# Input loads as steps of the planned order in the last stage of a graph network kernel

## The chip, the cores and the metric

The kernel runs on one core of a Trainium2 chip. The metric is the device time of one launch in microseconds; the figure to compare is the median of several runs. The engines are PE (matrix multiply), ACT (activations), DVE (vector operations), POOL (GpSimd) and SP (which only issues transfers here).

## The reference

x is 128 graphs of 128 nodes with 128 channels (float32); adj is a 0/1 adjacency matrix for each graph. Four layers follow one another, each of the form x = x + layer(relu(layernorm(x)), adj), and in each a softmax over a node's neighbours is taken.

```python
# --- layer 0: pairwise |xi - xj| scores, BatchNorm over all graphs, softmax, and then
y = (y - mg) / jnp.sqrt(vg + EPS) * gg + beg      # mg, vg over all graphs and nodes
y = _leaky(y)
out = jnp.concatenate([x, y], axis=2) @ Wt.T + bt
# --- layer 1: 8 heads of 32, then one head of 128 (masked softmax, ELU)
# --- layer 2: one head of 128 (masked softmax, ELU)
# --- layer 3: a bilinear score for each edge type, chosen by adj; softmax; two projections
```

Layer 0 needs means over all graphs, so everything up to y is done for all graphs first. What comes after y is separate for each graph: the rest of layer 0 and layers 1 to 3.

## The kernel before

The work falls into stages. First come the statistics of the pairs of nodes and the scores of layer 0; they leave in DRAM, for each group of 4 graphs (GC), four inputs of the last stage: xb (x with a bias, 256 KB), m (the mask, 128 KB), y (256 KB) and h (the normalised x, transposed, 256 KB). There are 32 groups. The last stage, `layers_01`, begins at about 1737 us. It takes a group from these four inputs to its output, through the rest of layer 0 and through layers 1, 2 and 3.

**A group's steps at the start**, with the lines of the profile: ACT makes yl from yt, scaled and shifted (L1866); DVE does the leaky step (L551); PE adds two products for each graph in po, ht times the first half of Wt and yl times the second (L1872, L1875); DVE adds xg and makes x1 (L1881); DVE takes mean and variance into mv (L1669, L1671); ACT makes the reciprocal root rs from them (L1674, L1675); POOL makes xn in two steps (L1678, L1679); PE transposes it (L1686) and ACT copies it out as hTc (L1689); PE projects it to pf (L1896); DVE splits pf in four instructions (L1905 to L1908) and ACT spreads the parts over heads as f1d and fl (L1917). On the side, DVE makes x1h (L1840). Then for each graph there are a product z (L1770), exponentials (L1776, L1779), the mask step p on DVE (L1781) and the sums (L1810). The output is written from SP at L2027.

**The order of the work.** Each group is a Python generator. Before a step it yields the engine, a cost in us, the buffers that the step takes and those that it frees. A list scheduler, `in_order` (L64), holds up to 8 groups under way (Z_UNDER_WAY), always picks the step that can begin first by these costs, and lets that generator emit its instructions. The order of emission is the order in which PE, ACT, DVE and POOL execute: each of these engines runs its instructions strictly in that order, and an instruction whose input has not come holds up those behind it. SP is not in that list (ORDERED): its requests are ordered by the framework. A step ends for its follower after a gap for its engine:

```python
AFTER = dict.fromkeys((PE, ACT, DVE, POOL), 0.2) | {DMA: 2.2}
...
begin = max([free_at[engine], c["ready"], *(events[e] for e in c["after"])])
```

Besides steps a generator can yield "fork" (start a side chain), "join" (go on when its side chains are done), "done" (set an event) and "after" (the next step waits for that event). Buffers are named: "ps" and "pz" are PSUM, "t", "w", "v" and others are SBUF tiles.

**The inputs.** `load` allocates xg, mask, yt and ht (3, 10, 3 and 3 buffers) and asks for them on SP in this order. It is a plain function: `group(g)` calls it for g + 1 when it starts, and neither the transfer nor its buffers appear in the plan. As eight groups start at plan time 0, the loads of groups 1 to 8 are written at the front. The inputs of group 0 lie in buffers of their own, filled before the stage (`first_in`).

Of the kernel before, what the change touches and what calls it, by code (L numbers as in the profile page):

```python
# [27 lines left out]
GC = 4  # L28
# [6 lines left out]
Z_T, Z_W, Z_P, Z_F, Z_O, Z_M = 30, 13, 4, 4, 6, 10  # L35
Z_KEPT = {"ps": 1, "t": 4, "w": 2, "v": 1, "vals": 1}
# [20 lines left out]
PE, ACT, DVE, POOL, DMA = "PE", "ACT", "DVE", "POOL", "DMA"  # L57
# [3 lines left out]
AFTER = dict.fromkeys((PE, ACT, DVE, POOL), 0.2) | {DMA: 2.2}  # L61
# [112 lines left out]
def kernel(ctx: ExitStack, tc: tile.TileContext, x, adj, w, out):  # L174
    nc = tc.nc
    NB = x.shape[0]
# [370 lines left out]
    def inputs_01(g):  # L547
        return xb_d[g], mask_d[g], y_d[g], h_d[g]
# [1080 lines left out]
    def layers_01(first_in):  # L1629

        with tc.tile_pool(name="c_in", bufs=3) as c_in, tc.tile_pool(
# [19 lines left out]
            def tile_t(name):  # L1651
                return c_t.tile([P, GC, P], F32, tag="t", name=name)
# [97 lines left out]
            loaded = dict(first_in)  # L1750

            def load(g):
                tiles = [
                    c_in.tile([P, GC, P], dtype, tag=name, name=name, bufs=n)
                    for name, dtype, n in (("xg", F32, 3), ("mask", BF16, Z_M), ("yt", F32, 3), ("ht", F32, 3))
                ]
                for dst, src in zip(tiles, inputs_01(g)):
                    nc.sync.dma_start(dst, src)
                loaded[g] = tiles

            def with_bias3(x3):
                yield POOL, 1.3, "", ""
                nc.gpsimd.tensor_tensor(x3, x3, bcast(pb_bc, 1, GC), ALU.add)
# [93 lines left out]

            def group(g):
                b0 = g * GC
                xg, mask, yt, ht = loaded.pop(g)  # L1860
                if g + 1 < NB // GC and g + 1 not in loaded:
                    load(g + 1)
                res = {}
                yield ACT, 0.72, "t", ""
                yl = tile_t("yl")
                nc.scalar.activation(yl, yt, AF.Identity, bias=y_bi, scale=y_sc)  # L1866
                yield DVE, 0.82, "", ""
# [3 lines left out]
                for i in range(GC):  # L1871
# [3 lines left out]
                    nc.tensor.matmul(  # L1875
                        po[:, i, :], yl[:, i, :], wtT[:, 1, :], start=False, stop=i == GC - 1
                    )
                yield "join",
                yield DVE, 0.66, "t", "ps"
                x1 = tile_t("x1")  # L1880
                nc.vector.tensor_tensor(x1, po, xg, ALU.add)  # L1881

# [20 lines left out]
                f = c_v.tile([P, 2 * P], BF16, tag="f", name="f")  # L1903
# [122 lines left out]
                nc.gpsimd.tensor_tensor(xh, xh, x3, ALU.add)  # L2026
                nc.sync.dma_start(out_t[:, b0 : b0 + GC, :], xh)  # L2027

            for g in range(2):
                if g not in loaded:  # L2030
                    load(g)
            in_order(
                [partial(group, g) for g in range(NB // GC)], Z_UNDER_WAY,
                {"ps": 4, "pz": 2, "t": Z_T, "w": Z_W, "vals": Z_P, "f": Z_F, "v": Z_O},
                Z_KEPT,
            )

    def layers(simple, first_in):
# [457 lines left out]
    with tc.If(nc.values_load(types[0:1, 0:1]) < 1) as only_01:  # L2496
        layers_01({0: early})
# [42 lines left out]
```

## Time and profile before

| | |
|---|---|
| median of 3 runs | 2680.19 us (2677.42 to 2680.2) |
| the profiled execution's own time | 2677.98 us |
| its span, with 51543 instructions | 2676.1 us |
| busy over the span: PE, DVE, ACT, POOL | 93%, 91%, 81%, 61% |
| DMA, mean over the span | 122.62 MB, 46 GB/s |
| last stage: first request of an input | 1736.98 us |
| last stage: first and last output request | 1868.64 and 2670.8 us |
| mean granted clock of PE | 0.972 |

The span is the time from the first to the last instruction of one profiled execution; its own time is 1.9 us longer. In rows of the trace a name such as "yl<-yt" says which tile is written from which. "Idle before, releaser" says how long the engine had done nothing before an instruction and which engine's result, or which transfer, ended that. In the views by stage, each engine has its busy time and its number of instructions, followed by the clock granted to PE (1 is full), the share of time in which the 16 DMA engines were busy, and GB/s.

### The profile page before, as it was taken

The numbers are of one execution on the slowest core, as the hardware profiler recorded it, in microseconds if no ns is written. First come the engines' busy times: TensorE is split into PE (matmuls) and PEld (weight loads), VectorE is DVE, ScalarE is ACT, GpSimd is POOL, SyncE is SP. The second block draws the span as 40 slices with busy tenths as digits, with TensorE's granted clock in tenths as the row PEclk, the third lists the DMA queues.
The fourth block names the chain that finished last, engine by engine and source line by source line (L and its number), as shares of the span: only waits on it lengthen the run. The fifth ranks groups of instructions, "written<-read, shape, count | busy, mean of one in ns | idle before, by whom it ended". The sixth has DMA issues, their size and how long they took to land. (4 is left out here: it accounts for less than half of the span.)

```text
span 2676.1 us, 51543 instructions
## 1 busy us (share of the span) xinstructions
PE 2489.0 (93%) x19585; PEld 1559.4 (58%) x19595; DVE 2423.4 (91%) x4638; ACT 2160.1 (81%) x3537; POOL 1632.1 (61%) x922
## 2 busy tenths in 40 slices
PE   8999999999999999799999999778998989898888
PEld 3433444444333333577777777566776767676766
DVE  9999999999999998889998998678988898889886
ACT  8999999999999998466665666468777777787885
POOL 8999999999999999544444443022333333333234
PEclk9999999999999999899999999979998999999999
DMA  3000000000000000322322221040211111110001
GB/s 103 24 24 24 24 24 24 24 24 24 24 24 24 24 23 21 113 86 83 100 92 88 88 84 44 22 133 10 62 35 48 37 37 45 46 45 25 10 2 34
DMA packets 135731, 122.62 MB, mean 46 GB/s; under 512 B 10865, under 2 KB 102450, under 8 KB 135474
## 3 DMA queue, kind: packets, MB, share of 16 engines
q1 hardware_dynamic: 134754, 118.89, 14.6%
q8 instruction: 158, 2.59, 0.4%
q14 instruction: 99, 0.81, 0.1%
q10 hardware_dynamic: 720, 0.33, 0.0%
HBM read 73.05 MB, written 46.14 MB: 45 GB/s over the span
## 5 line engine op out<-in xcount | busy, mean ns | idle before, releaser
L727 POOL TENSOR_TENSOR d<-he 128x2016 f32<-128x2016 f32 (+1 forms) x272 | 961.0, 3560 | 17.7 <-PE ph L752 14.2
L752 PE MATMUL ph<-d,w1T 128*64 128x512 f32 (+1 forms) x4096 | 912.7, 596 | 16.3 <-DVE six L764 9.8
L731 ACT ACTIVATE d<-d 128x2048 f32<-128x2048 f32 (+1 forms) x448 | 833.1, 1888 | 18.0 <-POOL d L727 17.0
L752 PEld LDWEIGHTS ph<-d,w1T 128*64 128x64 f32 x4096 | 322.8, 136 | 545.8 <-issue 471.1
L722 DVE SCALAR_TENSOR_TENSOR d<-pt,he 128x2048 f32<-128x2048 f32 x240 | 543.2, 2271 | 4.6 <-PE ph L752 4.4
L764 DVE BATCH_NORM_STATS2 six<-ph 128x6 f32<-128x512 f32 (+1 forms) x704 | 438.0, 677 | 11.7 <-PE ph L752 11.4
L1678 POOL TENSOR_TENSOR xn<-xo,mv 128x512 f32<-128x512 f32 x64 | 74.0, 1156 | 324.0 <-DVE mv L1671 257.1
L1083 PE MATMUL pl<-its,it 128*128 128x128 f32 x1280 | 171.4, 282 | 2.8 <-DVE its L1076 2.7
L758 ACT ACTIVATE ph<-ph 128x1008 f32<-128x1008 f32 x160 | 159.7, 998 | 11.9 <-PE ph L752 11.6
L1083 PEld LDWEIGHTS pl<-its,it 128*128 128x128 f32 x1280 | 155.5, 194 | 20.7 <-DVE its L1076 7.9
L1781 DVE SCALAR_TENSOR_TENSOR p<-z,mask 128x1024 f32<-128x1024 f32 x124 | 147.7, 1210 | 8.0 <-ACT z L1779 7.7
L1037 ACT ACTIVATE d<-diff 128x640 f32<-128x640 f32 x128 | 89.7, 701 | 79.4 <-PE diff L1028 79.4
L1679 POOL TENSOR_TENSOR xn<-xn,rs 128x512 f32<-128x512 f32 x96 | 110.9, 1155 | 51.3 <-ACT rs L1675 39.5
L1015 POOL TENSOR_TENSOR base<-base,own_d 128x512 f32<-128x512 f32 x32 | 43.4, 1357 | 158.3 <-PE ph L1041 77.4
L1073 ACT CAST it<-pi 128x640 f32<-128x640 bf16 x128 | 86.6, 691 | 64.7 <-PE pi L1070 64.7
L1028 PE MATMUL diff<-inc,h 128*128 128x320 bf16 x768 | 128.6, 304 | 5.8 <-DVE inc L944 3.9
L1779 ACT ACTIVATE z<-z 128x1024 f32<-128x1024 f32 x128 | 129.0, 1008 | 4.1
L944 DVE SCALAR_TENSOR_TENSOR inc<-in_row,row 128x8 bf16<-128x8 f32 (+12 forms) x512 | 126.0, 315 | 1.9 <-PE in_row L935 1.8
L1045 ACT ACTIVATE z<-ph,h_bi,h_sc 128x320 f32<-128x320 f32 x128 | 77.9, 618 | 54.4 <-PE ph L1041 52.5
L1678 POOL TENSOR_TENSOR xn<-x,mv 128x512 f32<-128x512 f32 x32 | 37.0, 1157 | 136.9 <-DVE mv L1671 72.6
L1810 PE MATMUL va<-p,vals 128*32 128x128 f32 x2048 | 107.6, 283 | 8.3 <-DVE vals L1795 4.9
L1076 DVE TENSOR_TENSOR its<-pi,s 128x640 f32<-128x640 bf16 x128 | 102.2, 809 | 13.1 <-ACT it L1073 12.7
(326 smaller groups left out, 5309.3 us busy)
## 6 DMA issues: line engine op xcount, KB each, us to landing
ht<-h SPq DMA_DIRECT2D x64, 256.0 KB, 2.7
n<-ln_xn SPq DMA_DIRECT2D x32, 256.0 KB, 2.4
h<-he SPq DMA_DIRECT2D x32, 256.0 KB, 2.6
adj<-in_adj SPq DMA_DIRECT2D x32, 256.0 KB, 3.0
xn<-n SPq DMA_DIRECT2D x32, 256.0 KB, 2.6
xb<-in_x SPq DMA_DIRECT2D x32, 256.0 KB, 3.0
xb<-xb SPq DMA_DIRECT2D x32, 256.0 KB, 2.0
xg<-xb SPq DMA_DIRECT2D x32, 256.0 KB, 2.7
```

What stands on the lines that cost most here:

```text
L722: nc.vector.scalar_tensor_tensor(dv, own, 0.0, later, ALU.max, ALU.max if is_larger else ALU.subtract)
L727: nc.gpsimd.tensor_tensor(dv, later, own, ALU.subtract)
L731: nc.scalar.activation(d[:, 0 : 4 * n], d[:, 0 : 4 * n], AF.Abs, accum_out=sums[:, g, k : k + 1] if on_act else None,)
L752: nc.tensor.matmul(ph[64 * a : 64 * a + 64, t, 0:n], wt, x_, start=part == 0, stop=not is_larger or part == 3,)
L758: nc.scalar.activation(ph[:, :, 0:n], ph[:, :, 0:n], AF.Square, accum_out=squares[:, g, k : k + 1])
L764: nc.vector.bn_stats(six[g][:, 2 * by_bn.index((i, q)) + t, :], ph[:, t, 0:n])
L944: nc.vector.scalar_tensor_tensor(inc[:, :, e : e + n], in_row[:, :, 0:n], float(k + 1), row[:, :, 0:n], ALU.is_equal, ALU.subtract,)
L1028: nc.tensor.matmul(diff[:, a, 0 : SLOT_N // 2], h[:, i, :], inc[:, a * SLOT_N // 2 : (a + 1) * SLOT_N // 2], start=m == 0, stop=m == 2,)
L1083: nc.tensor.matmul(made["pl"][:, i, :], it[:, k, :], its[:, k, :], start=k == 0, stop=k == 4)
L1678: nc.gpsimd.tensor_tensor(xn, x, bcast(mv[:, :, 0], 2, P), ALU.subtract)
L1779: nc.scalar.activation(z, z, AF.Exp, scale=1.0 - SLOPE)
L1781: nc.vector.scalar_tensor_tensor(p, z, 1.0, bcast(mask[:, i, :], 1, NH), ALU.max, ALU.mult)
```

## The change

All of it lies in `layers_01`. `load` becomes a side chain with a step of its own on an engine "DMA" of the plan: it costs 2.9, takes a buffer "in", of which there are three, and sets the event ("loaded", g) at its end. `group(g)` forks the load of g + 1; groups other than 0 wait in the plan for their own event before their first step, and give "in" back with x1. The order of the four requests becomes yt, ht, xg, mask. The "join" ahead of x1 is dropped. The loop that called `load(1)` before planning goes, and the plan takes ACT as free only from 1.5.

```diff
             def load(g):
+                yield DMA, 2.9, "in", ""
                 tiles = [
                     c_in.tile([P, GC, P], dtype, tag=name, name=name, bufs=n)
                     for name, dtype, n in (("xg", F32, 3), ("mask", BF16, Z_M), ("yt", F32, 3), ("ht", F32, 3))
                 ]
-                for dst, src in zip(tiles, inputs_01(g)):
-                    nc.sync.dma_start(dst, src)
+                parts = list(zip(tiles, inputs_01(g)))
+                for k in (2, 3, 0, 1):
+                    nc.sync.dma_start(*parts[k])
                 loaded[g] = tiles
+                yield "done", ("loaded", g)
...
             def group(g):
                 b0 = g * GC
-                xg, mask, yt, ht = loaded.pop(g)
-                if g + 1 < NB // GC and g + 1 not in loaded:
-                    load(g + 1)
+                in_slot = "" if g in first_in else "in"
+                if in_slot:
+                    yield "after", ("loaded", g)
+                if g + 1 < NB // GC:
+                    yield "fork", load(g + 1)
                 res = {}
                 yield ACT, 0.72, "t", ""
+                xg, mask, yt, ht = loaded.pop(g)
                 yl = tile_t("yl")
...
-                yield "join",
-                yield DVE, 0.66, "t", "ps"
+                yield DVE, 0.66, "t", "ps " + in_slot
                 x1 = tile_t("x1")
                 nc.vector.tensor_tensor(x1, po, xg, ALU.add)
...
-            for g in range(2):
-                if g not in loaded:
-                    load(g)
             in_order(
                 [partial(group, g) for g in range(NB // GC)], Z_UNDER_WAY,
-                {"ps": 4, "pz": 2, "t": Z_T, "w": Z_W, "vals": Z_P, "f": Z_F, "v": Z_O},
-                Z_KEPT,
+                {"ps": 4, "pz": 2, "t": Z_T, "w": Z_W, "vals": Z_P, "f": Z_F, "v": Z_O, "in": 3},
+                Z_KEPT, dict.fromkeys(AFTER, 0.0) | {ACT: 1.5},
             )
```

## The prediction, made before the changed kernel was run

> **What bounds the kernel now.** I read the page for the shares, then busy time by stage, then the waits of the last stage's first 25 us, then ACT and DVE there in order of time. Busy time by stage (each engine: us, instructions):
>
> ```profile
> core 0: us, PE busy (x) PEld busy (x) DVE busy (x) ACT busy (x) POOL busy (x), PEclk, DMA share, GB/s
> 1736.50:1749.00 12.50, 9.38 (x41) 8.82 (x42) 2.39 (x4) 4.53 (x5) 0.00 (x0) 0.51 0.77 261
> 1749.00:1761.00 12.00, 5.95 (x48) 5.76 (x48) 9.34 (x40) 4.68 (x11) 3.45 (x4) 0.78 0.95 294
> 1761.00:1773.00 12.00, 8.30 (x99) 6.06 (x99) 10.73 (x29) 9.25 (x22) 7.68 (x7) 0.78 0.28 92
> 1773.00:1783.00 10.00, 8.50 (x87) 5.56 (x87) 9.41 (x20) 9.74 (x19) 1.04 (x1) 0.67 0.09 26
> 1783.00:2640.00 857.00, 757.00 (x8387) 598.11 (x8386) 750.53 (x1670) 676.16 (x1488) 288.23 (x264) 0.95 0.12 33
> 2640.00:2676.10 36.10, 26.45 (x178) 21.31 (x176) 15.98 (x35) 14.84 (x28) 14.44 (x14) 0.92 0.17 47
> ```
>
> From 1783 to 2640 the stage runs on compute: PE 88%, DVE 88%, DMA 12%. The first 25 us are the reverse: DMA 77 to 95%, DVE 2.39 us of 12.5. Waits from 1736.5 to 1761 (total, times, longest):
>
> ```profile
> POOL xn L1678 <- DMA ht<-h: 17.3, 1, 17.3
> ACT yl L1866 <- DMA yt<-y: 13.4, 7, 3.3
> DVE yl L551 <- ACT yl L1866: 10.9, 5, 3.5
> DVE x L1881 <- DMA xg<-xb: 2.3, 1, 2.3
> ```
>
> By the tile views these are nearly all the waits for inputs in the stage: yt has only those seven. The mechanism is in the order of time (start, duration; ACT, then DVE):
>
> ```profile
> 1738.03 0.81 ACT L1866 ACTIVATE yl<-yt,y_bi,y_sc 128x512 f32<-128x512 f32 x1
> ...
> 1754.95 0.81 ACT L1866 ACTIVATE yl<-yt,y_bi,y_sc 128x512 f32<-128x512 f32 x1 [2.71 <-DMA yt<-y]
> 1757.13 0.81 ACT L1866 ACTIVATE yl<-yt,y_bi,y_sc 128x512 f32<-128x512 f32 x1 [1.37 <-DMA yt<-y]
> 1757.85 0.28 ACT L1674 ACTIVATE rs<-mv,eps_c 128x4 f32<-128x4 f32 x1
> ```
> ```profile
> 1749.29 0.68 DVE L1881 TENSOR_TENSOR x<-po,xg 128x512 f32<-128x512 f32 x1
> 1750.35 0.69 DVE L551 SCALAR_TENSOR_TENSOR yl<-yl 128x512 f32<-128x512 f32 x1 [0.38 <-ACT yl L1866]
> 1750.96 0.86 DVE L1669 BATCH_NORM_STATS2 s<-x 128x6 f32<-128x128 f32 x4
> 1751.74 0.36 DVE L1671 BATCH_NORM_AGGREGATE mv<-s 128x2 f32<-128x6 f32 x4
> ```
>
> The planner takes inputs as present, so it lays eight yl in a row on ACT (8 x 0.72 = 5.8 us by its costs). On the chip each waits for its yt. Group 0's rs needs only mv, done at 1752.1, but stands behind the eighth yl until 1757.85; its x1 stands behind the leaky steps of groups 1 to 3 until 1749.29, though its matmuls end near 1743.0.
>
> **The change, part by part.** *Removed:* the plan with eight yl in front. *Added:* no instruction and no transfer; 31 loads of four remain, and "after loaded" is a rule of the plan, not a semaphore. What an engine executes is the same in number and shape, so all of the effect is order.
>
> *yt and ht first.* yt of group 1 was third in the queue, behind 256 + 128 KB. At the 298 GB/s of 1740 to 1760 that is 1.3 us: 1741.27 becomes about 1740.0, and groups 2 and 3 (1745.42, 1747.84) move by the same to 1744.1 and 1746.5. xg and mask land up to 512 KB, 1.7 us, later in exchange: xg is read last at 1743, when it has come; mask of group 1 only at 1783. Cost nothing; if x1 were ready sooner, up to 1.7 us.
>
> *Loads as steps.* In plan time (0 is about 1736.5) the inputs of groups 1, 2, 3 are there at 5.1, 8.0 and 10.9 (2.9 each, then 2.2), that is 1741.6, 1744.5, 1747.4: close behind the landings just worked out, so ACT should stall less than 1 us. Group 4 waits for a slot, freed by x1 of group 1 near 10: 10.2 + 5.1 = 15.3. So yl comes every 3 to 3.3 us and rs, hTc and f1d go between. SP itself isn't bound to this order: yt was requested ten times by 1757.97, before the first output left at 1868.64, though the tenth load is written behind the end of group 1. What is requested when is thus set by free buffers, and each group's four requests (0.32 to 0.42 us each, 1.5 us) lie on SP beside compute, against 29 us for a group. The output stores on SP are waited for by nobody in a way the views show. For xg of group 4, requested at 1755.73 behind masks and yt of later groups, the trace can't say where it goes: 0 if it follows the earlier x1, up to 4 us if it still lands at 1760.7 when the plan wants x1 near 1756.5. I take 0.5 us, since masks of far groups come later in the text now.
>
> *What then moves.* Group 0: po ends 1743.0, x1 1743.1 (was 1749.29); statistics 0.68 + 0.86 + 0.36 end near 1744.8; rs 0.5; POOL's second step ends at about 1746.9 (was 1759.55). What is late next is PE: it takes 3.4 us for a group's po while its clock is low, so DVE gets 2.6 us of work (0.69 + 0.68 + 1.22) for each 3.4 us, 76%. From 1750, when group 0 brings x1h (0.68) and the split (1.8), DVE is full.
>
> *The sum*, by work done. Before, DVE had done 2.39 + 9.34 + 10.73 = 22.5 us by 1773, ACT 4.53 + 4.68 + 9.25 = 18.5. After, DVE: 1.4 by 1743.1; 0.76 x 6.9 = 5.2 by 1750; the other 15.9 at the stage's 0.876 take 18.2: 1768.2, so 4.8 ahead. ACT: four yl and two rs, 4.3 by 1750; 14.2 at 0.86 (18.99 of 22 in 1761 to 1783) take 16.5: 1766.5, so 6.5 ahead. Between them 5.7. Less 0.5 for xg, plus 1 for the low clock (next part): 6.2. The price of the old stalls is more (13.4), but a pipeline being filled has to wait for something.
>
> *ACT begins at 1.5 in the plan.* The table load is 1.28 us at 1736.73 in the trace, present before and after. It only makes the plan true: 0. Dropping the first "join" has no child to wait for: 0. The later join now waits, in the plan, for the next group's load; that load began some 15 us ahead and takes 5.1: 0, and 5 us in that group if it were late.
>
> *The clock.* In the trace a pair of po matmuls took 0.64 us from 1740 to 1748.6, 0.39 until 1753.4; PE then sat idle for 6.0 us and ran at 0.64 again until 1779.3. The Trainium skill ("TensorE: Matmul & The Clock Gate", Part 1) says some 3.4 us of sustained work frees the clock and long gaps throttle it. This speaks against the change: one dense block of eight po warms PE, spread ones may not. By the rule po at low clock for all eight groups costs PE 8 x 1.6 = 13 us more, in a stretch where DVE waited for PE only 1.2 us and ACT 2.3. By the trace the long release (9 us, not 3.4) was thrown away by the 6 us gap, which the change fills: gain of up to 2.3, or loss of about 3 if PE becomes the bound. I take a gain of 1.
>
> Against the profiled execution, 2677.98 (span 2676.1 and 1.9 around it): 2677.98 - 6.2 = 2671.8. The median is 2.2 above it: **2674**.
>
> **Rivals.** *Fill gain kept* (the forecast, 0.42): 2668 to 2677; the bounds above give 3 to 11 us.
> *Gain lost within the pipeline* (0.23). Against: groups are eight under way, so a head start isn't needed by anyone at once; outputs leave 8 to 41 us apart (2233.12 and 2240.65; 1956.67 and 1997.33), so there is slack. The order of 1783 to 2640 comes from the same list and may put the 6 us back as waits. Or the change doesn't do what it says: if ACT's order stayed and only the queue's order changed, 1.3 us. Time 2678 to 2681.
> *Worse order in the long stretch* (0.20), the other side. All later choices follow from which step was free first, so new starts mean a new order for 29 groups. DVE idles 857 - 750.5 = 106.5 us there, 3.7 us a group. 0.21 us more in each eats the 6.2; from 0.4 us (11%) the kernel is slower by 0.2%. At 0.6: 2674 + 17 = 2691. For it: PE waits for DVE p (20.9) and DVE for PE po (15.3) depend on order alone. Against: the costs and buffers of that stretch are the same.
> *Better order there* (0.15): the same mechanism, 0.35 us less a group: 2664; with less idle in the last 36 us too (DVE 15.98 busy), 2658.
>
> **How the numbers follow.** About 0.2% (5.4 us) is what a measurement of this kernel can tell from no change: faster is below 2674.8, slower above 2685.6. Faster: 0.35 of the forecast's 0.42 as most of its range lies below, and 0.15: 0.50. Slower: 0.20 and 0.02 from lost gains with a late xg: 0.22. The rest, 0.28, is the same. The range 2659 to 2688 leaves out 0.05 below and 0.13 above. The forecast's own is 2668 to 2677.
>
> **What would show it.** Right: rs of group 0 near 1746 instead of 1757.85; seven waits of yl for yt falling from 13.4 to under 4 us; DVE over 4.5 us busy in the first 12.5; the first mask step p near 1760 instead of 1772.98; the first output 5 to 8 us before 1868.64. Wrong: yl still in a row; DVE waiting over 4 us for xg; a pair of matmuls at 0.64 beyond 1780; or all of the fill as forecast while 1783 to 2640 needs more DVE idle time than 106 us.

## The result, and the profile after

The change makes the kernel slower by a little: 2684.33 us (median of 14 runs, 2675.88 to 2689.25) against 2678.94 us for the kernel before (14 runs, 2674.79 to 2680.29). The ratio is 1.002, 95% interval 1.0011 to 1.0028. The forecast was 2674, 10 us below that, although the point that I had reasoned about, the start of the stage, came out as forecast or better.

In its profiled execution the changed kernel took 2679.3 us with a span of 2677.1. There the stage began 4.15 us sooner than in the one before (table load at 1732.58 instead of 1736.73; in all profiled executions here it lies between 1732.6 and 1740.0, and the code ahead of it is the same in all). So I compare by distance from that load: the stage takes 939.4 us before and 944.5 after, 5.1 more, close to the difference of the medians (5.4).

First the fill. These are the stages shown of before, moved by 4.15 us (per engine: us, instructions; then clock, DMA share, GB/s):

```profile
1732.35:1744.85 12.50, 8.89 (x56) 8.22 (x57) 6.34 (x23) 5.71 (x10) 2.93 (x3) 0.75 0.80 274
1744.85:1756.85 12.00, 8.47 (x74) 6.63 (x73) 9.64 (x30) 9.34 (x20) 5.52 (x5) 0.81 0.73 241
1756.85:1768.85 12.00, 9.88 (x168) 6.52 (x167) 11.79 (x24) 11.71 (x24) 2.46 (x3) 0.90 0.26 89
1768.85:1778.85 10.00, 6.54 (x54) 5.23 (x53) 9.89 (x14) 9.69 (x17) 0.66 (x1) 0.87 0.19 55
```

DVE has 6.34 us of work in the first 12.5 instead of 2.39, and ACT has twice its work in the second (9.34 for 4.68). From the start of the stage to two later moments:

```profile
1732.35:1760.00 27.65, 20.52 (x152) 16.58 (x152) 18.95 (x57) 18.14 (x35) 9.48 (x8) 0.76 0.73 247
1732.35:1764.00 31.65, 24.01 (x224) 19.19 (x225) 22.92 (x62) 22.04 (x43) 9.48 (x8) 0.79 0.69 233
```

The waits of the first 24.5 us in the changed kernel:

```profile
POOL xn L1678 <- DMA ht<-h: 10.6, 1, 10.6
ACT L1638 <- DVE types L1183: 5.3, 1, 5.3
...
ACT yl L1872 <- DMA yt<-y: 3.3, 2, 2.6
```

Two waits for yt are left of seven, 3.3 us of 13.4, and none for xg. In order of time on ACT one sees why; lines 1866 and 1881 of before are 1872 and 1886 here:

```profile
1732.58 1.28 ACT L1638 ACT_TABLE_LOAD   x1 [5.30 <-DVE types L1183]
1733.88 0.81 ACT L1872 ACTIVATE yl<-yt,y_bi,y_sc 128x512 f32<-128x512 f32 x1
1735.43 0.81 ACT L1872 ACTIVATE yl<-yt,y_bi,y_sc 128x512 f32<-128x512 f32 x1 [0.74 <-DMA yt<-y]
1738.79 0.81 ACT L1872 ACTIVATE yl<-yt,y_bi,y_sc 128x512 f32<-128x512 f32 x1 [2.55 <-DMA yt<-y]
1741.26 0.30 ACT L1674 ACTIVATE rs<-mv,eps_c 128x4 f32<-128x4 f32 x1 [1.66 <-DVE mv L1671]
```

rs of group 0 follows the third yl, 8.7 us after the table load; before it was the ninth thing on ACT, at 21.1. DVE in the same kernel has x1 of group 0 at 6.3 (12.6 before) and the first mask step p at 23.1 (36.3):

```profile
1738.88 0.69 DVE L1886 TENSOR_TENSOR x<-po,xg 128x512 f32<-128x512 f32 x1 [3.41 <-PE po L1881]
...
1755.72 1.22 DVE L1784 SCALAR_TENSOR_TENSOR p<-z,adj 128x1024 f32<-128x1024 f32 x1 [2.12 <-ACT z L1782]
```

Then the end. I cut the stage at the moment when the last of the 32 groups starts (its yl, the last one in the trace), once in each kernel. Busy time by stage, the kernel before and then the changed one:

```profile
1736.70:2501.60 764.90, 667.94 (x7352) 528.89 (x7352) 661.66 (x1476) 599.90 (x1303) 250.23 (x229) 0.94 0.16 47
2501.60:2676.10 174.50, 147.64 (x1483) 116.73 (x1481) 136.72 (x317) 119.29 (x267) 64.60 (x59) 0.93 0.05 15
```
```profile
1732.60:2485.00 752.40, 664.65 (x7350) 526.30 (x7351) 639.15 (x1468) 595.94 (x1299) 248.43 (x227) 0.94 0.16 47
2485.00:2677.10 192.10, 153.38 (x1485) 120.37 (x1483) 143.36 (x325) 123.58 (x272) 69.34 (x61) 0.92 0.05 14
```

The counts in brackets make the cut fair: up to it both have done nearly the same (7352 and 7350 matmuls, 1476 and 1468 DVE instructions), and nearly the same is left (1483 and 1485, 317 and 325). For the first part the changed kernel needs 12.5 us less. For the second, the drain, in which the groups under way end and none takes the place of one that is done, it needs 17.6 us more: 12.5 - 17.6 = -5.1. DVE shows the drain's loss: 192.1 - 143.4 = 48.7 us idle instead of 37.8.

In the first part, on the other hand, DVE was not idle for less time but for more: 752.4 - 639.15 = 113.3 us instead of 103.2. That part is shorter because DVE was busy for 22.5 us less, with 8 instructions fewer of 1476. An instruction of one form does not always take the same time. In the kernel before, the leaky step took 0.69 us at 1750.35, and 1.49 here, beside an instruction of POOL:

```profile
1752.49 1.04 POOL L1678 TENSOR_TENSOR xn<-x,mv 128x512 f32<-128x512 f32 x1 [17.29 <-DMA ht<-h]
1752.60 1.49 DVE L551 SCALAR_TENSOR_TENSOR yl<-yl 128x512 f32<-128x512 f32 x1
```

Over all 32 groups the leaky step took 0.965 us in the mean before and 0.771 in the changed kernel. So the 12.5 us are not the gain of the fill alone: with the new order DVE's instructions also took less time.

### The profile page after: what moved, and what is told of

It is laid out like the page before. It is cut to its first block, busy times and chain, and to the rows that moved or that the text cites. A ratio compares the mean times of both kernels' runs of the same rounds, so it can differ in the third digit from the quotient of the medians.

```text
span 2677.1 us, 51563 instructions
## 1 busy us (share of the span) xinstructions
PE 2487.8 (93%) x19595; PEld 1558.9 (58%) x19595; DVE 2408.9 (90%) x4638; ACT 2160.3 (81%) x3537; POOL 1635.1 (61%) x922
## 4 chain that ended last, share of the span: by engine, by line
PE 52%; DVE 34%; ACT 7%; issue 4%; POOL 2%; DMA 0%; ACTq 0%; DVEq 0%; SPq 0%; POOLq 0%
PE ph L752 17%; DVE d L722 9%; DVE six L764 7%; PE pl L1083 5%; PE diff L1028 4%; PE ph L1041 2%; DVE p L1784 2%; PE sp L1051 2%; PE ph L1945 2%; DVE s L1669 2%; PE po L1738 2%; ACT d L731 2%; PE va L1813 1%; DVE xh L1747 1%; PE sm L1813 1%
## 5 line engine op out<-in xcount | busy, mean ns | idle before, releaser
L2031 POOL TENSOR_TENSOR xh<-xh,xo 128x512 f32<-128x512 f32 x32 | 45.5, 1423 | 168.3 <-DVE xh L1747 124.9
L1813 PE MATMUL va<-p,vals 128*32 128x128 f32 x2048 | 111.8, 291 | 13.9 <-DVE vals L1798 13.4
L1076 DVE TENSOR_TENSOR its<-pi,s 128x640 f32<-128x640 bf16 x128 | 102.2, 809 | 11.6 <-ACT it L1073 11.2
```

The lines of the kernel that those rows point to most:

```text
L1813: nc.tensor.matmul(to[rows, a, s, :], vals[:, NH * a + e, :] if to is va else es[:, i, e : e + 1].to_broadcast([P, DH]), ps_[i][:, e, :], ...
```

## The experiments

Two theories had to be told apart. **Order:** the steps make the plan of the fill true, but a list scheduler that begins otherwise lays all later steps otherwise, and this order happens to be worse. **Queue and slots:** the new requests, or three slots, hold up inputs somewhere. A number that the kernel itself has is of help: the time at which its own `in_order` places the last step of the stage, by the costs in the yields. It is 920.2 in the kernel before and 933.6 in the changed one. It is no time of the chip; the runs say how far the chip follows it.

**Requests alone.** The kernel before, with the loop of `load` changed and nothing else:

```diff
-                for dst, src in zip(tiles, inputs_01(g)):
-                    nc.sync.dma_start(dst, src)
+                parts = list(zip(tiles, inputs_01(g)))
+                for k in (2, 3, 0, 1):
+                    nc.sync.dma_start(*parts[k])
```

> The kernel before, with the four requests in the order yt, ht, xg, mask and nothing else changed; the plan is that of before. Order theory (the loss is a worse order of the later steps, chosen by the list scheduler): about 1 us faster than before, near 2678. Queue theory (the loss comes from the new order of the requests, xg and mask being late somewhere): slower than before by about the 5 us that the change lost, near 2684.

Measured: 2677.26 us against 2678.32 (ratio 1.000, 0.9992 to 1.0008). The queue is not where the time went; the gain of 1 us can't be told from none.

**Steps, with the old requests:**

```diff
-                for k in (2, 3, 0, 1):
+                for k in (0, 1, 2, 3):
```

> The changed kernel, with the requests back in the order xg, mask, yt, ht. Order theory: as the changed kernel, 2684, at most 2 us more. Queue theory: back at the time of before or below it, 2679 or less.

Measured: 2685.97 (1.0021, 1.001 to 1.0032), as the change. The loss is in the steps. These two kernels also repeat the cut, as their engines execute in the same order as those of before and of the change. The requests alone first, then the steps with the old requests:

```profile
1740.00:2500.40 760.40, 662.90 (x7352) 523.67 (x7353) 660.80 (x1476) 599.71 (x1304) 249.88 (x229) 0.95 0.16 47
2500.40:2674.70 174.30, 147.59 (x1482) 116.64 (x1481) 136.66 (x317) 119.35 (x267) 64.62 (x59) 0.94 0.06 16
```
```profile
1736.70:2488.40 751.70, 663.72 (x7350) 526.34 (x7350) 639.31 (x1468) 595.66 (x1298) 247.89 (x227) 0.94 0.16 47
2488.40:2680.90 192.50, 153.32 (x1485) 120.36 (x1483) 143.39 (x325) 123.70 (x272) 69.34 (x61) 0.92 0.05 14
```

The drain comes out the same to 0.4 us (174.3 after 174.5, 192.5 after 192.1). DVE's busy time over the stage repeats to 0.9 us: 797.5 after 798.4 without the steps, 782.7 after 782.5 with them. The first part repeats less well (760.4 after 764.9 with one order). Each kernel without the steps set against each with them gives a lead of 8.0 to 13.2 us at the last group's start.

**Four slots:**

```diff
-                {"ps": 4, "pz": 2, "t": Z_T, "w": Z_W, "vals": Z_P, "f": Z_F, "v": Z_O, "in": 3},
+                {"ps": 4, "pz": 2, "t": Z_T, "w": Z_W, "vals": Z_P, "f": Z_F, "v": Z_O, "in": 4},
```

> The changed kernel with 4 slots "in" in the plan instead of 3 (the tiles in memory stay at 3). The kernel's own list scheduler, read at its end, places the last step at 933.6 us in the changed kernel, at 920.2 in the kernel before and at 921.2 here. Order theory: the 12.4 us shorter plan is kept with the better fill, near 2672, faster than both. Slot theory (three slots or late loads hold groups back on the chip): faster too, but only as far as waits for inputs go, which the trace after puts at 3.3 us in all: 2681 or more.

Measured: 2668.52 (0.9961, 0.9948 to 0.9974), faster than both kernels. That is 15.8 us below the change, five times the 3.3 us of waits for yt that were left. And those waits did not go: they are 3.2 us here.

**ACT free from 0:**

```diff
-                Z_KEPT, dict.fromkeys(AFTER, 0.0) | {ACT: 1.5},
+                Z_KEPT,
```

> The changed kernel with ACT free from 0 in the plan instead of 1.5, as it was before. Slots, loads and requests are as in the changed kernel; the plan's own end becomes 946.0 instead of 933.6. Order theory: some 12 us slower than the changed kernel, near 2696. Queue and slot theories: as the changed kernel within 1.5 us, 2683 to 2686.

Measured: 2701.62 (1.009, 1.0075 to 1.0104). A start value of 1.5 us in the plan is worth 17.3 us of time. No computation, load or request differs in kind or number; queue and slots can't explain this. The expected size was 12, so the plan's end is not the whole of it. Nor is the drain always the place of the loss. Cut at the last group's start, this kernel gives:

```profile
1740.00:2515.40 775.40, 672.74 (x7474) 531.02 (x7475) 664.73 (x1519) 606.82 (x1320) 255.96 (x236) 0.95 0.15 46
2515.40:2699.80 184.40, 146.37 (x1360) 113.34 (x1359) 124.59 (x274) 114.89 (x251) 57.84 (x53) 0.90 0.05 14
```

More has been done at the cut (7474 matmuls for the 7350 of the change), so the parts can't be set off against each other exactly. But the first part is 23.0 us longer than in the change and the drain 7.7 shorter.

**The stage cut short.** To see where along the stage the loss arises, both kernels with fewer groups (16, and 30; the outputs of the others are left out), so that the drain falls elsewhere:

```diff
-                [partial(group, g) for g in range(NB // GC)], Z_UNDER_WAY,
+                [partial(group, g) for g in range(16)], Z_UNDER_WAY,
```

and the same bound for the load of g + 1.

> The kernel before with only 16 of the 32 groups in the last stage; the outputs of the other 16 are left out. It is the base for the next kernel. All theories: about 445 us shorter than before (plan 475.1 instead of 920.2), near 2234.

> The changed kernel with only 16 of the 32 groups in the last stage; the other 16 are left out. The plan's own end is 476.8, 1.7 us above that of before with 16 groups, where with 32 groups it is 13.4 above. Order theory (the fill gains 8 us or more against the plan; what is lost comes from the order of later groups): 5 to 9 us faster than before with 16. Queue and slot theories: the loss grows with the number of groups, so half of it, 2 to 3 us slower, or at best the same.

> The kernel before with only 30 of the 32 groups in the last stage; two groups are left out. Base for the next kernel. The plan's own end is 861.5 instead of 920.2: near 2620.

> The changed kernel with only 30 of the 32 groups in the last stage; two groups are left out. The plan's own end is 893.0, 31.5 above that of before with 30 groups. Order theory: 31.5 less the 8 us that the fill gives, some 20 to 24 us slower than before with 30. Queue and slot theories: as with 32 groups, about 5 us slower.

Measured: 2239.11 and 2222.15 with 16 groups, the change 17.0 us faster; 2621.27 and 2639.68 with 30, the change 18.4 us slower. With two groups more, 32, it loses only 5.4. A cost for each group can't turn from -17.0 to +18.4 and back to +5.4. With 16 the gain was about twice the upper end of what I expected (5 to 9).

**The plan's cost of a load, with four slots.** Last, a change that is nothing but a number in the plan (3.5 in a second kernel):

```diff
-                yield DMA, 2.9, "in", ""
+                yield DMA, 3.0, "in", ""
```

> The kernel with four slots, with 3.0 instead of 2.9 as the plan's cost of a load: no transfer, request or instruction differs, only the order. The list scheduler's own end goes from 921.2 to 906.9. Over the nine kernels with 32 groups, or fewer, run so far, the time was the plan's end plus 1745 to 1764, and 1745 to 1751 where ACT begins at 1.5. Order theory: 906.9 + 1748 = 2655. Rival (the four slots helped because inputs come earlier, the order of later steps doesn't matter): as with 2.9, 2668, within 2 us.

> The kernel with four slots and 3.5 as the plan's cost of a load. The list scheduler's own end is 953.2. Order theory: 953.2 + 1748 = 2701, slower than before and than the change, although its loads are planned with more room. Rival (inputs decide): 2668 to 2670.

(The kernels run by then were ten, not nine, and the old requests had given 1752.4, so the upper end for ACT at 1.5 was 1752.) Measured: 2653.05 with 3.0 (0.9916, 0.9899 to 0.9933), the fastest with 32 groups, and 2706.52 with 3.5 (1.0116, 1.0101 to 1.0132), the slowest: 53.5 us for 0.5 us of a planned cost. Inputs don't decide it: ACT waited 5.1 us for yt in the fastest of the two and 0.8 in the slowest. The stage of each, cut at the last group's start again, 3.0 first:

```profile
1733.00:2482.70 749.70, 662.89 (x7471) 527.26 (x7472) 662.84 (x1509) 606.72 (x1325) 256.45 (x233) 0.96 0.16 48
2482.70:2649.60 166.90, 140.64 (x1364) 111.20 (x1362) 129.72 (x284) 111.62 (x246) 61.36 (x55) 0.93 0.06 16
```
```profile
1733.50:2488.60 755.10, 655.33 (x7176) 518.15 (x7177) 644.46 (x1471) 586.29 (x1281) 249.40 (x231) 0.95 0.16 47
2488.60:2700.60 212.00, 166.33 (x1657) 130.70 (x1655) 147.08 (x322) 134.21 (x289) 61.73 (x57) 0.88 0.05 13
```

The last group starts at nearly the same distance, 749.7 and 755.1, but with 3.0 more has been done by then (1509 DVE instructions for 1471, 7471 matmuls for 7176), and the drain takes 166.9 us instead of 212.0. DVE idles 37.2 us in the one drain and 64.9 in the other.

All kernels together (us):

| kernel | plan's own end | median | difference |
|---|---|---|---|
| before | 920.2 | 2678.9 | 1758.7 |
| requests alone | 920.2 | 2677.3 | 1757.1 |
| before, 16 groups | 475.1 | 2239.1 | 1764.0 |
| before, 30 groups | 861.5 | 2621.3 | 1759.8 |
| the change | 933.6 | 2684.3 | 1750.7 |
| old requests | 933.6 | 2686.0 | 1752.4 |
| four slots | 921.2 | 2668.5 | 1747.3 |
| ACT free from 0 | 946.0 | 2701.6 | 1755.6 |
| change, 16 groups | 476.8 | 2222.2 | 1745.4 |
| change, 30 groups | 893.0 | 2639.7 | 1746.7 |
| four slots, cost 3.0 | 906.9 | 2653.1 | 1746.2 |
| four slots, cost 3.5 | 953.2 | 2706.5 | 1753.3 |

The chip follows the plan, to some us. Without the steps it is 1757 to 1764 us longer than its plan (mean 1759.9), with them and ACT at 1.5 it is 1745 to 1753 (mean 1748.9 of seven). I read the 11 us between the means as what the steps bring, since the plan is true with them, and the plan's own end as what they cost: +13.4 here. 13.4 - 11.0 = 2.4; measured 5.4, as these differences scatter by 4 us to either side. This reading is not shown by a run of its own, and the 11 is rough: with 32, 30 and 16 groups the steps' kernel beats its plan by 8.0, 13.1 and 18.6 us more than the one without.

## Why the prediction was wrong

- **What bounds the fill:** right. The seven waits fell to two, x1 of group 0 came 6.3 us after the table load (6.4 forecast), rs 8.7 (about 9), the first p 23.1 (about 23).
- **yt and ht first:** right. Expected 1.3 us, measured 1.1 and not clear of zero.
- **xg of group 4:** I took 0.5 with up to 4; it was 0, as DVE waits for no xg. The requests followed the earlier x1.
- **The sum by work done:** right for the fill. DVE reached its 22.5 us of work 31.2 us into the stage's shifted window instead of 36.5, 5.3 ahead (4.8 worked out); ACT its 18.5 about 8.5 ahead (6.5 worked out). The first output left 117.4 us after the table load instead of 131.9, 14.5 sooner (5 to 8 forecast). The lead was still there at the last group's start, where it was 12.5, so the "gain lost within the pipeline" didn't take place up to then. What of the 12.5 is the fill and what the later order isn't separated.
- **The clock:** the granted share over the first four stretches is 0.75, 0.81, 0.90 and 0.87 (moved by 4.15 us), above the 0.51, 0.78, 0.78 and 0.67 of before, so the sign was right. But low stretches remain: po pairs took 0.64 us until 1738.7 and again from 1753.7 to 1757, and the sums at 1781 were slow once more after a wait of 3.5 us, the sign beyond 1780 that I had named for a wrong step. What the 1 us that I took was really worth wasn't tried alone. I also misread the clock before: it was not at 0.64 without a break until 1779.3, as po pairs took 0.39 from 1762.56 to 1763.01.
- **The step that failed** is the last one: from the lead in the fill to the end of the kernel, "2677.98 - 6.2". It took for granted that the later steps cost what they cost before. In the runs the lead was there until the last group started, and then the drain took 17.6 us more (18.2 with the other pair of kernels). I had written that "new starts mean a new order for 29 groups" and gave a worse order 0.20, a better one 0.15, so I had the cause; but I gave it too small a price and the wrong place. I priced it as DVE idle time for each group in 1783 to 2640 (0.6 us a group for the worst case). The sign that I had named did come: in the same stretch of the changed kernel, moved by 4.15 us, DVE idles 857 - 726.5 = 130.5 us instead of 106.5.

```profile
1778.85:2635.85 857.00, 753.61 (x8300) 596.35 (x8299) 726.52 (x1655) 663.95 (x1464) 288.52 (x261) 0.94 0.12 34
```

But DVE idle time was the wrong measure, as DVE's busy time wasn't fixed: over the stage it fell by 15.9 us (798.4 to 782.5) for the same instructions, and at the last group's start the changed kernel was ahead. The spread between orders is 53.5 us in these runs, three times the 17 of that rival. A change of the plan should have been forecast with a range of that width around a fill gain, and with the chance of slower near that of faster.
- The slack that I read from the outputs was misread too: in the trace of before they leave up to 46.6 us apart (2240.65 and 2287.29), not 41.
- Against the order there was one argument, that "the costs and buffers of that stretch are the same". The runs refute it: the kernels with 3.0 and 3.5 have the same buffers and the same work for the chip.

What stays open is why a given order drains badly. The plan's end foretells the total roughly, but no run here changed the drain alone. The dropped "join" and the wait for a load's event were not tried apart from each other either.

## What to carry to other kernels

Where a greedy list scheduler (one that always takes the step that can begin first) fixes the order, a change to its inputs has two effects: what it was made for, and a throw of the dice for everything placed later. Here, by the table, the first was a gain of about 11 us and the second +13.4. To value such a change, vary a meaningless number in the plan a few times (a cost by 0.1, which was worth 15.5 us with four slots) and compare the spread with the gain; then keep the best order, for which the plan's own end is a usable guide. To find where a lead is lost, cut both traces at equal work, by counts of instructions, not at equal times.

## What the runs showed of the hardware

**The clock of PE** was released after different times. The po matmuls that begin the stage went from 0.64 to 0.39 us a pair after 3.2 us in the changed kernel (1735.53 to 1738.68), and after 8.9 in the kernel before (1739.68 to 1748.6, with one pause of 0.7 us; counted from its end, 1743.75, it is 4.85). The changed kernel first:

```profile
1738.25 0.59 PE L1881 MATMUL po<-w_T,yl 128*128 128x128 f32 x2
1738.68 0.39 PE L1878 MATMUL po<-w_T,ht 128*128 128x128 f32 x2
```
```profile
1748.60 0.49 PE L1875 MATMUL po<-w_T,yl 128*128 128x128 f32 x2
1748.92 0.39 PE L1872 MATMUL po<-w_T,ht 128*128 128x128 f32 x2
```

The Trainium skill ("TensorE: Matmul & The Clock Gate", Part 1) speaks of some 3.4 us of sustained work, which fits the first and not the second, counted either way.

**DVE beside POOL.** In the kernel before, 86 of DVE's 1792 instructions in the stage took over 1.25 times as long as the quicker ones of their line, 58 us more in sum; in the changed kernel it was 77, and 45 us. Each of them overlaps an instruction of POOL; of the 1232 and 1142 that overlap none, not one is slow. Overlap alone is not enough: 474 and 573 overlap one and are not slow. No run here changes the overlap alone, so what else is needed stays open.

**The spread of runs.** The changed kernel's first 14 runs spread more than those of before (13.4 us for 5.5), along with the granted clock: 2675.88 us at 0.976, 2689.25 at 0.968. But 26 later runs of the kernel before spread by 11.2 us, so this isn't shown to come from the change.
